# Attention over halves of the scores: the maximum in two parts on VectorE, and the scaled values on GpSimd

## The chip, the cores and the metric

The kernel runs on one core of one Trainium2 chip. The metric is the device time of one execution in microseconds (us); lower is better. Times given for a kernel are medians of several executions. The core has five engines that run their own queues of instructions in order: TensorE (PE, with its weight loads as PEld), VectorE (DVE), ScalarE (ACT), GpSimd (POOL) and SyncE (SP). They wait for each other by semaphores.

## What is computed

Two layers over x of shape 8 x 256 x 32 x 32, so 8 batches of 1024 tokens with 256 channels. The change lies in the attention of layer 0, which has 8 heads of 64 channels and takes its softmax over the queries (axis i), not over the keys:

```
qkv = (xt @ w_qkv + b_qkv).reshape(B, S, N_HEADS, 3 * D_K)
q, k, v = jnp.split(qkv, 3, axis=-1)
attn = jnp.einsum('bihd,bjhd->bijh', q, k) * SCALE
attn = jax.nn.softmax(attn, axis=1)
res = jnp.einsum('bijh,bjhd->bihd', attn, v).reshape(B, S, N_HEADS * D_K)
res = res @ w_out + b_out + xt
```

Layer 1 is an attention with one head over normalized tokens (`_L1_attn_ref`), added to its input, and a mixture of 8 experts, of which each token takes 2 (`_L1_ffn_ref`), added again.

## The kernel before

The outer loop runs over the 8 batches. A batch goes through `layer0` (the attention with 8 heads), `attend` (the attention of layer 1) and `dispatch` (router, ranks, and the scatter of the normalized tokens into a table of rows by expert: 16 indirect transfers on POOL's queue at line 610, and an addition on POOL at line 617). The batches form two groups, 0 to 6 and 7. When a group's last batch has been dispatched, `experts` runs its blocks of 256 rows. Its results are fetched back token by token in `results`: indirect transfers on POOL at line 800, products and sums on DVE at line 806, transposes on PE at line 817. For batches 0 to 6 this is done inside the `layer0` of batch 7.

In `layer0` the softmax axis is the queries. So the scores are made transposed: a tile has 128 keys on the partitions and 1024 queries along the free axis, and the maximum and the sum are taken along the free axis. There are 4 pairs of heads (g) and 8 blocks of 128 keys (j), so 32 steps (g, j) per batch. In a step:

- `score(at, h, n)`, line 323: one matmul for head h of the pair and half n (512 queries). Head 0 uses rows 0 to 63 of the array and head 1 rows 64 to 127, so matmuls of different heads run side by side. A score tile `psc` takes two PSUM banks, one for each half; there are 3 such buffers (`ps_big`).
- `soften(at, h)`: the negated maximum over 1024 queries on DVE (line 334), the exponential on ACT with the sum as accumulator output (line 336), and, for h = 1, the reciprocals of both sums (line 343) and the values times the reciprocals, `vs` (line 345), both on DVE.
- `gather_values(at)`, line 361: four matmuls that add the products of `vs` and the exponentials into `po`, two steps later (`LAG = 2`).

The loop at line 373 writes the order out by hand: the first half of head 0 stands beside the second half of head 1 of the step before, then the second half of head 0 beside the first half of head 1. After steps 3 and 5 of a pair, `project` (line 272, evicted on DVE at line 280) makes a query or key tile for the next pair in a buffer of the same pool. A scheduler places the instructions of each engine from this program, and puts in the semaphore waits.

Of the kernel before, what the change touches and what calls it, by code (L numbers as in the profile page):

```python
# [10 lines left out]
F32 = mybir.dt.float32  # L11
I32 = mybir.dt.int32
AF = mybir.ActivationFunctionType
ALU = mybir.AluOpType
AX = mybir.AxisListType
# [3 lines left out]
def kernel(  # L19
# [21 lines left out]
    nc = tc.nc  # L41
    P = 128
# [17 lines left out]
    const = ctx.enter_context(tc.tile_pool(name="const", bufs=1))  # L60
# [4 lines left out]
    small = ctx.enter_context(tc.tile_pool(name="small", bufs=6))  # L65
# [95 lines left out]
    nc.gpsimd.memset(later[:, :, 0:1], 0.0)  # L161

    wpack = dram.tile([E * P, WROW], F32, name="wpack")
    wbs = [const.tile([P, WROW], F32, name=f"wb_{i}") for i in range(NWB)]


    ps = acc("ps_bqk")
# [4 lines left out]
    ps = acc("ps_W")  # L172
# [7 lines left out]
    ps = acc("ps_r")  # L180
# [4 lines left out]
    ps = acc("ps_b1")  # L185
# [116 lines left out]
    def layer0(b, xT, between):  # L302

        v = values(b, xT)
        res = one.tile([P, NPAIR, S], F32, tag="res", name=f"res_{b}")
        qks = [[project(b, xT, 0, t) for t in range(2)]]
        if b == 0:  # L310
            prepare()
        steps = [(g, j) for g in range(NPAIR) for j in range(NT)]
        LAG = 2
        pss, exps, sums, vss = {}, {}, {}, {}
        po = None

        def score(at, h, n):
            g, j = steps[at]
            q, k = qks[g]
            if n == 0:  # L320
                pss[at, h] = big(f"psc_{b}_{g}_{j}_{h}")
            r = slice(h * DK, (h + 1) * DK)
            nc.tensor.matmul(  # L323
                pss[at, h][:, ts(n, 512)], k[r, ts(j, P)], q[r, ts(n, 512)], start=True, stop=True
            )

        def soften(at, h):

            g, j = steps[at]
            ps = pss.pop((at, h))  # L330
            if h == 0:
                sums[at] = small.tile([P, 2], F32, tag="sums", name=f"sums_{b}_{g}_{j}")
            nmax = small.tile([P, 1], F32, tag="nmax", name=f"nmax_{b}_{g}_{j}_{h}")
            nc.vector.tensor_reduce(nmax, ps, AX.X, ALU.max, negate=True)  # L334
            ex = expp.tile([P, 1024], F32, tag="exps", name=f"ex_{b}_{g}_{j}_{h}")
            nc.scalar.activation(  # L336
                ex, ps, AF.Exp, bias=nmax, scale=1.0, accum_out=sums[at][:, h : h + 1]
            )
            exps[at, h] = ex
            if h == 1:  # L340

                rs = small.tile([P, 2], F32, tag="rs", name=f"rs_{b}_{g}_{j}")
                nc.vector.reciprocal(rs, sums.pop(at))
                vs = four.tile([P, 2, DK], F32, tag="vs", name=f"vs_{b}_{g}_{j}")
                nc.vector.tensor_mul(  # L345
                    vs,
                    v[:, j, ts(g, P)].rearrange("p (h d) -> p h d", d=DK),
                    rs.unsqueeze(2).to_broadcast([P, 2, DK]),
                )
                vss[at] = vs  # L350

        def gather_values(at):
            nonlocal po
            g, j = steps[at]
            if j == 0:
                po = [acc(f"po_{b}_{g}_{n}") for n in range(NH2)]
            vs = vss.pop(at)
            exs = [exps.pop((at, h)) for h in range(2)]
            for n in range(NH2):
                for h in range(2):  # L360
                    nc.tensor.matmul(  # L361
                        po[n][h * DK : (h + 1) * DK, :],
                        vs[:, h, :],
                        exs[h][:, ts(n, 512)],
                        start=(j == 0),
                        stop=(j == NT - 1),
                    )
            if j == NT - 1:
                for n in range(NH2):
                    nc.scalar.copy(res[:, g, ts(n, 512)], po[n])  # L370

        last = len(steps) - 1
        for at in range(last + LAG + 1):
            if at <= last:
                score(at, 0, 0)
            if 0 < at <= last + 1:
                score(at - 1, 1, 1)
                soften(at - 1, 1)
            if at <= last:
                score(at, 0, 1)  # L380
                score(at, 1, 0)
                soften(at, 0)
            if at >= LAG:
                gather_values(at - LAG)
            if at <= last:
                g, j = steps[at]
                if j == NT - 1:
                    for group, item in between[g]:
                        results(group, [item])
                if g + 1 < NPAIR and j in (3, 5):  # L390
                    if j == 3:
                        qks.append([])
                    qks[g + 1].append(project(b, xT, g + 1, len(qks[g + 1])))


        t1 = one.tile([P, NT, C], F32, tag="t1", name=f"t1_{b}")
        for i in range(NT):
            pr = acc(f"pr_{b}_{i}")
            for g in range(NPAIR):
                nc.tensor.matmul(  # L400
                    pr[:, :C], res[:, g, ts(i, P)], wo[:, g, :], start=(g == 0), stop=False
                )
            for cc in range(NCC):
                nc.tensor.matmul(
                    pr[:, ts(cc, P)], xT[:, cc, ts(i, P)], ident, start=False, stop=(cc == NCC - 1)
                )
            nc.vector.tensor_add(t1[:, i, :], pr[:, :C], b_o)
        return t1


    def attend(b, t1):
        n1 = one.tile([P, NT, D], F32, tag="n", name=f"n1_{b}")
        layer_norm(t1, n1, 1e-5, f"a{b}")
        nT = one.tile([P, NCC, S], F32, tag="nT", name=f"nT_{b}")
        to_channels(n1, nT, f"n1_{b}")
        xa = one.tile([P, NCC, S], F32, tag="xa", name=f"xa_{b}")
        for ec in range(NCC):
            px = big(f"px_{b}_{ec}")
            for dc in range(NCC):
                for n in range(NH2):  # L420
                    nc.tensor.matmul(  # L421
                        px[:, ts(n, 512)],
                        WT[:, dc, ts(ec, P)],
                        nT[:, dc, ts(n, 512)],
                        start=(dc == 0),
                        stop=(dc == NCC - 1),
                    )
            nc.vector.tensor_copy(xa[:, ec, :], px)

        t2 = t1  # L430

        def scores(i):
            psc = big(f"ps1_{b}_{i}")
            for ec in range(NCC):
                for n in range(NH2):
                    nc.tensor.matmul(  # L436
                        psc[:, ts(n, 512)],
                        xa[:, ec, ts(i, P)],
                        nT[:, ec, ts(n, 512)],
                        start=(ec == 0),  # L440
                        stop=(ec == NCC - 1),
                    )
            nmax = small.tile([P, 1], F32, tag="nmax", name=f"nmax1_{b}_{i}")
            nc.vector.tensor_reduce(nmax, psc, AX.X, ALU.max, negate=True)  # L444
            ex = expp.tile([P, 1024], F32, tag="exps", name=f"ex1_{b}_{i}")
            ssum = small.tile([P, 1], F32, tag="ssum", name=f"ssum_{b}_{i}")
            nc.scalar.activation(ex, psc, AF.Exp, bias=nmax, scale=1.0, accum_out=ssum)  # L447
            return ex, ssum

        def mix(i, ex, ssum):  # L450
            pt = big(f"pa_{b}_{i}")
            for m in range(NT):
                nc.tensor.transpose(pt[:, ts(m, P)], ex[:, ts(m, P)], ident)
            aT = two.tile([P, S], F32, tag="tr", name=f"aT_{b}_{i}")
            nc.vector.tensor_copy(aT, pt)  # L455
            py = acc(f"py_{b}_{i}")
            for m in range(NT):
                nc.tensor.matmul(  # L458
                    py[:, :D], aT[:, ts(m, P)], n1[:, m, :], start=(m == 0), stop=(m == NT - 1)
                )  # L460
            rs = small.tile([P, 1], F32, tag="rs1", name=f"rs1_{b}_{i}")
            nc.vector.reciprocal(rs, ssum)
            nc.vector.scalar_tensor_tensor(  # L463
                t2[:, i, :], py[:, :D], rs, t1[:, i, :], ALU.mult, ALU.add
            )

        pending = None
        for i in range(NT):
            now = (i, *scores(i))
            if pending is not None:  # L470
                mix(*pending)
            pending = now
        mix(*pending)
        return t2
# [408 lines left out]
```

## Time and profile before

| | |
|---|---|
| median of 3 runs | 2899.07 us (2894.92 to 2901.2) |
| the profiled execution | 2900.13 us |
| its span, first to last instruction | 2898.4 us |
| mean granted TensorE clock | 0.943 |
| maximum over queries, line 334 | 512 instructions, 1219 ns each |
| exponentials, line 336 | 512 instructions, 1114 ns each |
| reciprocals, line 343 | 256 instructions, 165 ns each |
| values times reciprocals, line 345 | 256 instructions, 292 ns each |
| scatters, line 610 | 128 instructions on POOL, 974 ns each |

The profile is of one execution. Engines are named as above; "busy" is the time in which an engine runs an instruction. In the list of groups, a line gives the source line, the engine, the operation, what is written from what, the shapes and the count; after the first bar the busy time and the mean duration of one in ns; after the second the idle time of the engine just ahead of them and what ended most of it. In the timeline the columns are start, duration, engine, line and operation, and in brackets the idle time before and its releaser.

### The profile page before, as it was taken

The numbers are of one execution on the slowest core, as the hardware profiler recorded it, in microseconds if no ns is written. First come the engines' busy times: TensorE is split into PE (matmuls) and PEld (weight loads), VectorE is DVE, ScalarE is ACT, GpSimd is POOL, SyncE is SP. The second block draws the span as 40 slices with busy tenths as digits, with TensorE's granted clock in tenths as the row PEclk, the third lists the DMA queues.
The fourth block names the chain that finished last, engine by engine and source line by source line (L and its number), as shares of the span: only waits on it lengthen the run. The fifth ranks groups of instructions, "written<-read, shape, count | busy, mean of one in ns | idle before, by whom it ended". The sixth has DMA issues, their size and how long they took to land. (4 is left out here: it accounts for less than half of the span.)

```text
span 2898.4 us, 26495 instructions
## 1 busy us (share of the span) xinstructions
PE 2629.9 (91%) x10049; PEld 1379.7 (48%) x10049; DVE 1480.7 (51%) x2666; ACT 844.0 (29%) x1451; POOL 442.4 (15%) x445
## 2 busy tenths in 40 slices
PE   8999999999999999999999999999499988889946
PEld 3346434643464346434643464346377753224634
DVE  4664566456645664566456645664433335555422
ACT  2531253125312531253125312531011113332101
POOL 0000200020002000200020002000444442441043
PEclk9999999999999999999999999999699998879968
DMA  6984100010001000100010001000355532331044
GB/s 241 385 309 134 58 1 15 1 44 1 15 1 44 1 15 1 44 0 15 0 44 1 15 0 44 1 1 1 117 175 178 182 118 72 117 110 59 4 168 157
DMA packets 89304, 209.17 MB, mean 72 GB/s; under 512 B 16256, under 2 KB 22040, under 8 KB 87128
## 3 DMA queue, kind: packets, MB, share of 16 engines
q1 hardware_dynamic: 59272, 128.87, 12.3%
q0 software_dynamic: 29904, 78.61, 8.7%
q8 instruction: 79, 1.29, 0.2%
q14 instruction: 49, 0.40, 0.0%
HBM read 113.22 MB, written 126.36 MB: 83 GB/s over the span
## 5 line engine op out<-in xcount | busy, mean ns | idle before, releaser
L336 ACT ACTIVATE ex<-psc,nmax 128x1024 f32<-128x1024 f32 x512 | 570.5, 1114 | 846.8 <-DVE nmax L334 842.1
L334 DVE TENSOR_REDUCE nmax<-psc 128x1 f32<-128x1024 f32 x512 | 604.1, 1219 | 240.4 <-PE psc L323 240.2
L323 PE MATMUL psc<-qk,qk 64*128 64x512 f32 x2048 | 612.9, 645 | 35.4 <-DVE qk L280 20.7
L361 PE MATMUL po<-ex,vs 128*64 128x512 f32 x2048 | 508.8, 613 | 14.7 <-DVE vs L345 14.7
L323 PEld LDWEIGHTS psc<-qk,qk 64*128 64x128 f32 x2048 | 237.2, 191 | 377.6 <-ACT ex L336 162.0
L617 POOL TENSOR_TENSOR t<-t,n 128x2048 f32<-128x2048 f32 x8 | 36.1, 4511 | 1888.0 <-issue 1478.2
L361 PEld LDWEIGHTS po<-ex,vs 128*64 128x64 f32 x2048 | 127.2, 138 | 368.7 <-issue 307.5
L458 PE MATMUL py<-n,aT 128*128 128x256 f32 x1024 | 236.5, 384 | 11.2 <-DVE aT L455 11.2
L436 PE MATMUL ps<-nT,xa 128*128 128x512 f32 x512 | 236.9, 593 | 0.0
L272 PE MATMUL pqk<-xT,wqkv 128*128 128x512 f32 x512 | 233.9, 602 | 0.4 <-ACT ex L336 0.4
L458 PEld LDWEIGHTS py<-n,aT 128*128 128x128 f32 x1024 | 190.6, 190 | 67.3 <-DVE aT L455 43.9
L280 DVE TENSOR_SCALAR qk<-pqk,b_qk 128x1024 f32<-128x1024 f32 x64 | 82.1, 1283 | 180.3 <-PE pqk L272 180.3
L768 PE MATMUL pe<-wb,hb 128*128 128x256 f32 x624 | 156.1, 393 | 13.7 <-ACT hb L753 13.4
L447 ACT ACTIVATE ex<-ps,nmax 128x1024 f32<-128x1024 f32 x64 | 71.3, 1114 | 332.8 <-DVE nmax L444 325.1
L272 PEld LDWEIGHTS pqk<-xT,wqkv 128*128 128x128 f32 x512 | 93.4, 190 | 139.0 <-issue 99.2
L743 PE MATMUL ph<-xb,wb 128*128 128x256 f32 x624 | 152.7, 389 | 3.1 <-DVE xb L735 3.1
L800 POOL DMA_INDIRECT yk<-y,yat x128 | 123.8, 967 | 188.5 <-DVE o L806 97.4
L610 POOL DMA_INDIRECT rows<-n,d_at x128 | 124.6, 974 | 177.4 <-DVE row L597 125.5
L291 PE MATMUL pv<-wqkv,xT 128*128 128x512 f32 x256 | 142.0, 707 | 9.2 <-ACT wqkv L95 7.1
L753 ACT ACTIVATE hb<-ph,wb 128x256 f32<-128x256 f32 x156 | 65.5, 471 | 284.8 <-issue 241.2
L463 DVE SCALAR_TENSOR_TENSOR t<-py,rs,t 128x256 f32<-128x256 f32 x64 | 31.0, 484 | 228.2 <-PE py L458 228.2
L735 DVE COPY xb<-px 128x512 f32<-128x512 f32 x78 | 54.0, 692 | 157.5 <-PE px L733 157.5
(151 smaller groups left out, 2344.5 us busy)
## 6 DMA issues: line engine op xcount, KB each, us to landing
rows<-wb SPq DMA_DIRECT2D x8, 8192.0 KB, 51.3
y<-yb SPq DMA_DIRECT2D x78, 256.0 KB, 2.0
sums<-t SPq DMA_DIRECT2D x8, 1024.0 KB, 3.9
o<-sums SPq DMA_DIRECT2D x8, 1024.0 KB, 6.6
out_dram<-oT SPq DMA_DIRECT2D x16, 512.0 KB, 6.8
xT<-in_x_dram SPq DMA_DIRECT2D x7, 1024.0 KB, 6.0
wpack<-in_L_ffn_w_dram SPq DMA_DIRECT2D x4, 1024.0 KB
rows<-n,d_at POOLq DMA_INDIRECT x128, 2.4
```

The costliest lines, as they stand in the source:

```text
L272: nc.tensor.matmul(pq[:, ts(n, 512)], wqkv[:, cc, t, ts(g, P)], xT[:, cc, ts(n, 512)], start=(cc == 0), stop=(cc == NCC - 1),)
L291: nc.tensor.matmul(pv[:, ts(j, 512)], xT[:, cc, ts(i + j, P)], wqkv[:, cc, 2, :], start=(cc == 0), stop=(cc == NCC - 1),)
L323: nc.tensor.matmul(pss[at, h][:, ts(n, 512)], k[r, ts(j, P)], q[r, ts(n, 512)], start=True, stop=True)
L334: nc.vector.tensor_reduce(nmax, ps, AX.X, ALU.max, negate=True)
L336: nc.scalar.activation(ex, ps, AF.Exp, bias=nmax, scale=1.0, accum_out=sums[at][:, h : h + 1])
L361: nc.tensor.matmul(po[n][h * DK : (h + 1) * DK, :], vs[:, h, :], exs[h][:, ts(n, 512)], start=(j == 0), stop=(j == NT - 1),)
L436: nc.tensor.matmul(psc[:, ts(n, 512)], xa[:, ec, ts(i, P)], nT[:, ec, ts(n, 512)], start=(ec == 0), stop=(ec == NCC - 1),)
L458: nc.tensor.matmul(py[:, :D], aT[:, ts(m, P)], n1[:, m, :], start=(m == 0), stop=(m == NT - 1))
L610: nc.gpsimd.indirect_dma_start(out=view[:, :], out_offset=bass.IndirectOffsetOnAxis(ap=at[:, i : i + 1], axis=0), in_=n2[:, i, :], in_offs ...
L743: nc.tensor.matmul(ph[:, ts(fc, BR)], wb[:, dc * FF + fc * P : dc * FF + (fc + 1) * P], xb[:, dc, :], start=(dc == 0), stop=(dc == NCC - 1),)
L768: nc.tensor.matmul(py[:, ts(r, D)], hT[:, fc, ts(r, P)], wb[:, at + fc * D : at + (fc + 1) * D], start=(fc == 0), stop=(fc == NFC - 1),)
L800: nc.gpsimd.indirect_dma_start(out=yk[:, :], out_offset=None, in_=group.y[:, :], in_offset=bass.IndirectOffsetOnAxis(ap=ats[k][:, i : i + ...
```

## The change

The maximum of a score tile is taken in two parts. `first_max` reduces the first half (512 queries, one bank) with the same reduction as before. `soften` then runs one `tensor_scalar` over the second half: it multiplies by -1, takes the minimum with the first half's result, writes that to a scratch tile in SBUF that nobody reads, and gives the minimum over the free axis as its accumulator output. The score matmul of the second half would have to wait for `first_max`, because both use one tile; `declare_no_dep` tells the scheduler that they touch different banks, so no such wait is put in. `first_max` is called ahead of the second half's matmul. The product `vs` moves from DVE to POOL. In `attend` only the name of a tile changes.

```
+    scrap = const.tile([P, 512], F32, name="scrap")
...
-            nc.tensor.matmul(
+            mm = nc.tensor.matmul(
                 pss[at, h][:, ts(n, 512)], k[r, ts(j, P)], q[r, ts(n, 512)], start=True, stop=True
             )
+            if n == 1:
+                tc.declare_no_dep(mm.ins, firsts.pop((at, h)).ins, reason="the other bank")
+
+        def first_max(at, h):
+            g, j = steps[at]
+            nmax = small.tile([P, 1], F32, tag="nmax1", name=f"nmax1_{b}_{g}_{j}_{h}")
+            firsts[at, h] = nc.vector.tensor_reduce(
+                nmax, pss[at, h][:, ts(0, 512)], AX.X, ALU.max, negate=True
+            )
+            nmaxes[at, h] = nmax
...
-            nc.vector.tensor_reduce(nmax, ps, AX.X, ALU.max, negate=True)
+            nc.vector.tensor_scalar(
+                scrap,
+                ps[:, ts(1, 512)],
+                -1.0,
+                nmaxes.pop((at, h)),
+                ALU.mult,
+                ALU.min,
+                accum_out=nmax,
+            )
...
-                nc.vector.tensor_mul(
+                nc.gpsimd.tensor_mul(
                     vs,
...
             if at <= last:
+                first_max(at, 0)
                 score(at, 0, 1)
                 score(at, 1, 0)
                 soften(at, 0)
+                first_max(at, 1)
             if at >= LAG:
                 gather_values(at - LAG)
```

## The prediction

> **What bounds the kernel now.** The page comes first: which engine is full, and what the longest idle times of the others end on.
>
> ```profile
> PE 2629.9 (91%) x10049; PEld 1379.7 (48%) x10049; DVE 1480.7 (51%) x2666; ACT 844.0 (29%) x1451; POOL 442.4 (15%) x445
> L334 DVE TENSOR_REDUCE nmax<-psc 128x1 f32<-128x1024 f32 x512 | 604.1, 1219 | 240.4 <-PE psc L323 240.2
> ```
>
> TensorE (PE) works 91% of the span. The maximum that the change splits costs VectorE (DVE) 604 us, but DVE is half idle, so its busy time is no time to be won. What counts is the wait that ends last in the stage of the change. The timeline of a plain stretch of that stage (batch 1) shows it:
>
> ```profile
> 401.14 1.94 PE L361 MATMUL po<-ex,vs 128*64 128x512 f32 x8
> 403.01 2.17 PE L323 MATMUL psc<-qk,qk 64*128 64x512 f32 x8
> 404.18 2.36 DVE L334 TENSOR_REDUCE nmax<-psc 128x1 f32<-128x1024 f32 x2 [0.79 <-PE psc L323]
> 405.11 1.94 PE L361 MATMUL po<-ex,vs 128*64 128x512 f32 x8
> 405.50 1.11 ACT L336 ACTIVATE ex<-psc,nmax 128x1024 f32<-128x1024 f32 x1 [1.50 <-DVE nmax L334]
> 406.63 1.11 ACT L336 ACTIVATE ex<-psc,nmax 128x1024 f32<-128x1024 f32 x1
> 406.98 2.04 PE L323 MATMUL psc<-qk,qk 64*128 64x512 f32 x8
> 407.65 0.19 ACT L336 ACTIVATION_READ_ACCUMULATOR ex<-psc,nmax 128x1 f32 x1
> 407.89 0.29 PEld L323 LDWEIGHTS psc<-qk,qk 64*128 64x128 f32 x3 [0.19 <-ACT ex L336]
> 408.94 1.94 PE L361 MATMUL po<-ex,vs 128*64 128x512 f32 x8
> 410.81 2.17 PE L323 MATMUL psc<-qk,qk 64*128 64x512 f32 x8
> ```
>
> One step is a group of scores (L323) and a group of value products (L361). Two limits lie almost on each other. PE alone needs 1.96 us for a score group (406.98 to 408.94) and 1.87 for a value group (408.94 to 410.81): 3.83 a step. The other limit is a loop through three engines. From a group's start, 403.01, the first maximum starts 1.17 later and lasts 1.22; ScalarE (ACT) starts 0.10 after it, at 405.50, the second exponential follows at 406.63, and its accumulator is read by 407.84. Only then is its PSUM buffer free, and the second pair of scores of the next group starts at 407.89: 4.88 after 403.01. From there PE needs 2.92 to the group at 410.81. Two steps take 7.80, so 3.90 each. A shorter chain could save at most 0.07 a step.
>
> **The half maxima.** The order of instructions in the changed program keeps PE's sequence in batches 0 to 6, and its score matmuls wait for ACT alone, as before: the removed wait is the one that the new first maximum would have brought. DVE's order per step is: first half of (k, 0), second half of (k-1, 1), second half of (k, 0), first half of (k, 1), reciprocal. The matmuls that free the first two run as one pair and end together, so the useful second half stands behind a first half of another tile. Its rows:
>
> ```profile
> L654 DVE TENSOR_REDUCE p_e<-p_mine 128x63 f32<-128x504 f32 x1 | 0.7, 673 | 0.0
> L735 DVE COPY xb<-px 128x512 f32<-128x512 f32 x78 | 54.0, 692 | 157.5 <-PE px L733 157.5
> L617 POOL TENSOR_TENSOR t<-t,n 128x2048 f32<-128x2048 f32 x8 | 36.1, 4511 | 1888.0 <-issue 1478.2 <-DVE n L206 409.8
> ```
>
> First half: 0.68 (504 elements take 0.673), less 0.08 that two reductions in a row overlap (2.36 for two of 1.22): 0.60. Second half: between 0.69 (the copy of 512) and 0.75 (the tensor_scalar of line 280 takes 1.28 for 1024; 512 elements fewer save 0.53, the difference of copies of 1024 and 512, 1.225 and 0.692): 0.72. The accumulator output is not in the trace on DVE; on ACT the read adds 0.09 behind the activation. I take 0.09. Together 1.41 in place of 1.22: the chain is 0.19, say 0.2, **longer**. Bounds: 0.60 + 0.69 + 0 gives +0.07; 0.68 + 0.75, a whole small instruction of 0.17 (the reciprocal) and 0.04 for a wait on DVE's own semaphore give 1.64, +0.42. A gain is excluded here, since both halves wait for the same pair.
>
> The two-step loop becomes 7.80 + 0.2, so a plain step costs 0.10 more. A batch has 32 groups; between their starts lie 3 intervals of start-up, 6 pairs of 7.42 and 4.37 around the projections of line 272, and 16 plain ones of 3.90. The projection intervals absorb it: the group after a projection has 0.28 to 0.41 us to spare (at 426.61 PE starts, while the first exponential was read by 426.07). So 16 x 7 x 0.10 = **+11 us**. At +0.07 it is +4. At +0.42 another loop, group to first exponential to next group (2.49 + 1.21 + 0.05 = 3.75), becomes 4.17, 0.27 over 3.90: 30, and 4 more around projections, +34.
>
> [...]
>
> **The products on GpSimd (POOL).** In plain steps they are covered: a product is ready 0.39 us into the step that uses it (403.11 + 0.29) and PE takes it at 2.10 (405.11). Without that slack they would cost their own duration. What they are moved past is POOL's queue. In the changed order the products of batches 1 to 6 stand behind the 16 scatters of the batch before, and these run on into the new batch:
>
> ```profile
> 333.95 0.28 DVE L345 TENSOR_TENSOR vs<-v,rs 128x128 f32<-128x128 f32 x1
> 334.55 0.20 PEld L361 LDWEIGHTS po<-ex,vs 128*64 128x64 f32 x4 [1.30 <-DVE vs L345]
> 335.89 0.97 POOL L610 DMA_INDIRECT rows<-n,d_at  x1 [0.30 <-issue]
> ```
>
> The last scatter ends at 336.86, 2.31 after PE took the first product at 334.55; in batches 2 to 6 it is 2.34 to 2.43. The addition of line 617 stands ahead of the scatters in both orders. A product of 128 elements on POOL costs between 0.28 (4.511 x 128 / 2048) and 0.42 (with the 0.134 of POOL's smallest memset on top); I take 0.42, and 0.1 for hand-overs as between DVE and ACT. PE starts at 337.4, **2.85** late. Everything on PE stands behind it in order. While it waits, DVE and ACT stop too, for want of PSUM buffers, so nothing is caught up.
>
> The clock: after a 3.4 us stretch with PE 2.50 of 3.40 busy (327.4 to 330.8) the next stretch, 330.9 to 334.2, was granted 0.50, all others around it 1.00. A stall of 2.85 leaves PE emptier than that. A half-speed stretch costs up to 1.7; I take 1.2. Per batch 4.05, six times: **+24**. Low: 2.5 without the clock, +15; high: 2.85 + 0.6 + 1.7, +31.
>
> [...]
>
> **Ends of batches.** After the last group PE waits for a chain without cover (maximum at 474.57, value products at 477.76). There the second half alone stands on the path: 0.81 for 1.22, and the product 0.42 for 0.29. Net -0.28, eight times: **-2** (-3 to 0). The start of batch 0 gains and loses some 0.4.
>
> **Batch 7** takes gathered rows (line 800) through the same POOL queue, one each 1.26 us, and PE waits for them at lines 817. Some 12 of its 32 products stand between paced gathers, 0.7 each with the issue gap: 0 to 8. Two transposes also move back past score matmuls in PE's order, some us either way. I take **+3** (0 to 12).
>
> **Sum:** 11 + 24 - 2 + 3 = +36. The profiled execution took 2900.13 us, 1.7 around its span of 2898.4; the median is 2899.07, 1.1 below it, so I add to the median: **2935**. Low ends together: 4 + 15 - 3 + 0 = +16, 2915. High ends: 34 + 31 + 0 + 12 = +77, 2976.
>
> **Rivals.** (1) The start-up wait is hidden: POOL's scatters run earlier, or PE finds other work. Against it: the changed order puts nothing between. Then 11 - 2 + 3 = +12: 2911. (2) The chain is at its upper bound, because the accumulator read is a full instruction and DVE waits on itself, and batch 7 queues badly: 2960 to 2976. For it: the order shows the second half waiting for DVE as well as PE. (3) Faster: the mechanism is the split itself. If, in plain steps, DVE delivers the first maximum of a step earlier than after 1.22 us, that is, if both pieces together take less than that, the loop shrinks to PE's 3.83: 112 x 0.07 = -8, with -2 at the ends, -3 at the starts: 2886, provided POOL's wait stays away too. Against it: no 512-element row is below 0.67. (4) The change does nothing: the chain +0.07 and the wait hidden: about 2900.
>
> **Chances.** Forecast (2915 to 2955) 0.60; rival 1 0.12; rival 2 0.15; rival 3 0.06; rival 4 0.07. The time is the forecast's, 2935. The range reaches into rivals 1 and 2: 2908 to 2968. About 0.2%, 6 us, is what a measurement of this kernel can tell from no change. Faster 0.06, same 0.08 (rival 4 and the edge of rival 1), slower 0.86.
>
> **What would show it.** Plain steps of 4.00 instead of 3.90, with ACT's first exponential 2.7 after the group's start instead of 2.49. At the start of batches 1 to 6, PE idle about 3 us on a POOL product after the last scatter, and a further stretch at clock 0.5. The forecast is wrong if plain steps stay at 3.90 or fall, or if the first value group of batch 1 still starts about 9.2 us after its first scores.

## The result, and the profile after

| | before | after |
|---|---|---|
| median | 2897.05 us (4 runs, 2894.92 to 2901.2: the three above and one beside the changed kernel) | 2917.77 us (4 runs, 2913.8 to 2918.78) |
| ratio | | 1.0067, 95% interval 1.005 to 1.0085 |
| profiled execution, span | 2898.4 us | 2916.2 us |
| mean granted TensorE clock | 0.943 | 0.947 |

The change costs 20.7 us, 0.7%. These are the engines' line and the changed groups on the page of the changed kernel, and below them the group of value matmuls on the page of the kernel before:

```profile
PE 2631.1 (90%) x10049; PEld 1375.4 (47%) x10049; DVE 1481.8 (51%) x3434; ACT 837.4 (29%) x1451; POOL 544.1 (19%) x701
...
L382 PE MATMUL po<-ex,vs 128*64 128x512 f32 x2048 | 518.1, 624 | 35.4 <-POOL vs L366 35.4
L335 DVE TENSOR_REDUCE nmax<-psc 128x1 f32<-128x512 f32 x512 | 351.1, 687 | 260.4 <-PE psc L324 260.1
...
L347 DVE TENSOR_SCALAR_CACHE_REDUCE scrap<-psc,nmax 128x512 f32<-128x512 f32 x512 | 382.3, 747 | 59.8 <-PE psc L324 30.6
...
L366 POOL TENSOR_TENSOR vs<-v,rs 128x128 f32<-128x128 f32 x256 | 102.2, 401 | 1084.2 <-DVE rs L364 869.6
```

```profile
L361 PE MATMUL po<-ex,vs 128*64 128x512 f32 x2048 | 508.8, 613 | 14.7 <-DVE vs L345 14.7
```

Two pieces of the maximum take 687 and 747 ns where one took 1219, and DVE is as busy as before (1481.8 us against 1480.7), although 256 products of 0.29 us have left it. The line to look at is the first group: PE waits 35.4 us ahead of value matmuls, all of it for a product on POOL; before it was 14.7, for a product on DVE. In the trace, 23.1 of the 35.4 us lie at the starts of batches 1 to 6, where the kernel before has no such wait; the ends of batches and batch 7 hold the rest.

One of these starts, that of batch 1 after the change, in the timeline:

```profile
332.79 0.16 DVE L364 RECIPROCAL rs<-sums 128x2 f32<-128x2 f32 x1
...
333.31 0.96 POOL L633 DMA_INDIRECT rows<-n,d_at  x1 [0.30 <-DVE rs L364]
...
334.58 0.97 POOL L633 DMA_INDIRECT rows<-n,d_at  x1 [0.30 <-issue]
335.57 0.76 POOL L366 TENSOR_TENSOR vs<-v,rs 128x128 f32<-128x128 f32 x2
336.03 0.29 PEld L382 LDWEIGHTS po<-ex,vs 128*64 128x64 f32 x4 [4.55 <-POOL vs L366]
336.03 3.68 PE L382 MATMUL po<-ex,vs 128*64 128x512 f32 x8 [3.72 <-POOL vs L366]
...
341.66 0.69 DVE L335 TENSOR_REDUCE nmax<-psc 128x1 f32<-128x512 f32 x1 [8.12 <-PE psc L324]
```

Even the reciprocal of the second step has been there since 332.95. Two products stand behind POOL's last scatters, which end at 335.55, and run at once, 335.57, both together in 0.76. PE has waited 3.72 us. Then its eight matmuls take 3.68 where eight took 1.94 in a plain stretch before, and DVE gets its next scores 8.12 us after its last work. The windows of the granted clock over the same stretch (columns: window, its length, then PE's, PEld's, DVE's, ACT's and POOL's busy time with the number of instructions, granted TensorE clock, DMA share, GB/s) say why:

```profile
327.74:331.15 3.41, 2.98 (x8) 1.24 (x8) 3.19 (x9) 2.74 (x6) 2.50 (x4) 1.00 0.27 94
331.16:334.57 3.41, 1.15 (x5) 0.32 (x3) 2.12 (x5) 2.41 (x4) 2.50 (x3) 1.00 0.28 99
334.57:337.98 3.41, 1.95 (x6) 0.72 (x8) 0.00 (x0) 0.00 (x0) 1.73 (x3) 0.50 0.22 77
337.98:341.39 3.41, 3.41 (x10) 0.90 (x8) 0.00 (x0) 0.00 (x0) 0.00 (x0) 0.50 0.00 0
```

PE is busy 1.15 us of the stretch from 331.16, and the next two stretches are granted 0.50.

The plain steps of batch 1 after the change:

```profile
403.75 1.99 PE L324 MATMUL psc<-qk,qk 64*128 64x512 f32 x8
...
404.92 0.69 DVE L335 TENSOR_REDUCE nmax<-psc 128x1 f32<-128x512 f32 x1 [1.30 <-PE psc L324]
405.52 0.74 DVE L347 TENSOR_SCALAR_CACHE_REDUCE scrap<-psc,nmax 128x512 f32<-128x512 f32 x1
...
406.19 0.08 DVE L347 DVE_READ_ACCUMULATOR scrap<-psc,nmax 128x1 f32 x1
406.37 1.11 ACT L357 ACTIVATE ex<-psc,nmax 128x1024 f32<-128x1024 f32 x1 [1.93 <-DVE scrap L347]
...
407.48 1.10 ACT L357 ACTIVATE ex<-psc,nmax 128x1024 f32<-128x1024 f32 x1
407.63 0.30 PEld L324 LDWEIGHTS psc<-qk,qk 64*128 64x128 f32 x4 [0.90 <-ACT ex L357]
```

From the first piece to the first exponential it is now 1.45 us (404.92 to 406.37), against 1.32 before (404.18 to 405.50). The accumulator read is a row of its own, 0.08 us. The first exponential starts 2.62 after the group, where it was 2.49, and the next group, at 407.63, waits for it. Two plain steps take 7.89 (403.75 to 411.64) for 7.80.

To see where the time went as a whole, the span is cut by PE's records, for batches 0 to 6: from a batch's first scores to the start of its fourth group (start-ups), from there to its last group (the 28 later steps), from that to its last value matmul (ends), and from there to the next batch's first scores (gaps: the rest of layer 0, layer 1 and the router; six of them). The last column is the rest: batch 7, with the experts before and after it. About 38 us lie ahead of the first scores in each and are in no column. From its first scores to its last value matmul a batch is in its head, as it is called below.

| us | span | start-ups | later steps | ends | gaps | rest |
|---|---|---|---|---|---|---|
| before | 2898.4 | 77.8 | 932.2 | 66.7 | 814.8 | 968.6 |
| after | 2916.2 | 103.5 | 943.9 | 65.3 | 800.4 | 964.8 |
| split alone | 2883.4 | 70.0 | 940.4 | 63.9 | 806.3 | 964.5 |
| POOL products alone | 2916.6 | 103.3 | 932.7 | 68.3 | 802.8 | 971.0 |
| after, first products on DVE | 2891.4 | 70.0 | 940.2 | 65.4 | 812.1 | 965.6 |
| split alone, order turned | 2856.1 | 70.4 | 925.5 | 63.6 | 802.2 | 956.8 |
| the same, later products on POOL | 2864.6 | 70.4 | 925.6 | 65.1 | 799.9 | 965.1 |
| split at starts and ends only | 2880.2 | 70.0 | 934.3 | 64.8 | 803.8 | 969.4 |
| before, one matmul more | 2883.9 | 69.7 | 932.0 | 66.7 | 804.5 | 973.1 |
| before, delayed once | 2904.0 | 76.6 | 932.1 | 66.8 | 818.8 | 972.3 |
| before, again | 2900.0 | 76.7 | 932.0 | 66.7 | 815.2 | 972.0 |
| after, wait kept | 3138.6 | 113.7 | 1105.2 | 72.0 | 816.1 | 993.0 |

Between before and after, start-ups cost 25.7, later steps 11.7, ends give 1.4, gaps 14.3 and the rest 3.9: +17.8 in the spans (the medians differ by 20.7; this profiled execution of the kernel before is one of its longer ones). The gaps, whose code the change hardly touches, are the surprise.

### The profile page after: what moved, and what is told of

It is laid out like the page before. It is cut to its first block, busy times and chain, and to the rows that moved or that the text cites. A ratio compares the mean times of both kernels' runs of the same rounds, so it can differ in the third digit from the quotient of the medians.

```text
span 2916.2 us, 28469 instructions
## 1 busy us (share of the span) xinstructions
PE 2631.1 (90%) x10049; PEld 1375.4 (47%) x10049; DVE 1481.8 (51%) x3434; ACT 837.4 (29%) x1451; POOL 544.1 (19%) x701
## 5 line engine op out<-in xcount | busy, mean ns | idle before, releaser
L382 PE MATMUL po<-ex,vs 128*64 128x512 f32 x2048 | 518.1, 624 | 35.4 <-POOL vs L366 35.4
L335 DVE TENSOR_REDUCE nmax<-psc 128x1 f32<-128x512 f32 x512 | 351.1, 687 | 260.4 <-PE psc L324 260.1
L347 DVE TENSOR_SCALAR_CACHE_REDUCE scrap<-psc,nmax 128x512 f32<-128x512 f32 x512 | 382.3, 747 | 59.8 <-PE psc L324 30.6
L366 POOL TENSOR_TENSOR vs<-v,rs 128x128 f32<-128x128 f32 x256 | 102.2, 401 | 1084.2 <-DVE rs L364 869.6
L791 PE MATMUL pe<-wb,hb 128*128 128x256 f32 x624 | 156.1, 393 | 13.7 <-ACT hb L776 13.4
```

What stands on the lines that cost most here:

```text
L335: firsts[at, h] = nc.vector.tensor_reduce(nmax, pss[at, h][:, ts(0, 512)], AX.X, ALU.max, negate=True)
L347: nc.vector.tensor_scalar(scrap, ps[:, ts(1, 512)], -1.0, nmaxes.pop((at, h)), ALU.mult, ALU.min, accum_out=nmax,)
L382: nc.tensor.matmul(po[n][h * DK : (h + 1) * DK, :], vs[:, h, :], exs[h][:, ts(n, 512)], start=(j == 0), stop=(j == NT - 1),)
L791: nc.tensor.matmul(py[:, ts(r, D)], hT[:, fc, ts(r, P)], wb[:, at + fc * D : at + (fc + 1) * D], start=(fc == 0), stop=(fc == NFC - 1),)
```

## The experiments

Edits are against the kernel named. Ratios are to the kernel before, run beside it on the same chip: 2899.61 us for the first four experiments below, 2900.75 for the run with one matmul more and for the last one, 2901.96 for the others.

**The split alone** (the changed kernel with its product back on DVE):

```
-                nc.gpsimd.tensor_mul(
+                nc.vector.tensor_mul(
```

> The halves of the maximum as in the change, the products of values back on VectorE. My theory (two separate causes): the longer chain alone is here. Plain steps average 3.94 to 3.95 us as in the changed kernel, the steps with a projection 7.50 instead of 7.42, the first value products of batches 1 to 6 start at most 9.3 us after the first scores, since no product stands behind a scatter. The layer-0 heads grow by about 1 us each, 7 to 9 us in all without batch 7; what lies between the heads may give some of it back through the clock, 0 to 14 us. Time: 2890 to 2905. Rival (the wait for GpSimd is what lengthens the chain, through the reciprocal that waits on GpSimd): plain steps go back to 3.90.

Measured: 2886.21 us (2882.38 to 2889.84), ratio 0.9962, interval 0.9948 to 0.9977. The split by itself makes the kernel faster, and more so than expected. Its plain steps are slower, as in the changed kernel (112 of 3.94 instead of 3.90, +4.6, and 42 projection intervals of 7.50 instead of 7.42, +3.6); ends give 2.8 back, since only the second piece stands on their path; start-ups give 7.8 and gaps 8.5. Where these two come from is followed up below.

**The POOL products alone** (the kernel before with the product on POOL):

```
-                nc.vector.tensor_mul(
+                nc.gpsimd.tensor_mul(
```

> The maximum in one reduction as before, only the products of values on GpSimd. My theory: plain steps stay at 3.90 and projection steps at 7.42; in batches 1 to 6 the first value products start about 12.1 us after the first scores instead of 9.25, and the start-up (first three intervals) grows from 11.1 to about 15.5 us, 27 us in all. Between the heads the clock gives back 0 to 14 us. Time: 2908 to 2925. Rival (start-up is lost to the split order, not to the queue): start-up stays at 11.1 and the time at 2897.

Measured: 2917.61 us (2912.14 to 2921.45), ratio 1.0065, interval 1.0049 to 1.0081: the loss of the whole change. Start-ups of batches 1 to 6 take 15.0 to 15.6 us instead of 11.1; plain steps stay at 3.90. POOL's part is the loss and nothing but start-ups carries it. The two parts don't add: -13.4 and +18.0 would make +4.6, and the change has +20.7. What the split wins at a start-up is spent waiting for the same scatters: the start-ups are 103.3 without the split and 103.5 with it.

**The changed kernel with the products of a batch's first three steps on DVE:**

```
-                nc.gpsimd.tensor_mul(
+                mul = nc.vector if at < 3 else nc.gpsimd
+                mul.tensor_mul(
```

> The changed kernel with the products of the first three steps of each batch on VectorE and the other 29 on GpSimd. My theory: the start-up stall behind the scatters is gone, the first value products start at most 9.3 us after the first scores, start-up falls from 15.6 to 11.1 us or a little less; plain steps stay at 3.94. Time between 2890 and 2905. Rival (products on GpSimd cost in every step, or the scatters still hold the fourth product): start-up or the steps after it stay long and the time stays above 2908.

Measured: 2892.51 us (2887.82 to 2895.19), ratio 0.9977, interval 0.9967 to 0.9987. 24 of 256 products moved back take 25 us off. Start-ups are those of the split alone, 70.0, and the other 232 products cost 1.5 us at the ends (9.33 for 9.11 each) and nothing in the steps. Of the 24, the 18 in batches 1 to 6 stood behind scatters. So it is the queue behind the scatters, not POOL's slower product, that the change pays for. Batch 0, which has no scatters ahead of it, says the same inside the changed kernel's own trace: its start-up takes 9.95 us.

**The kernel before, delayed once** by some 2 us in batch 0, to see whether the gaps depend on where a batch falls on the grid on which the granted clock changes (in the clock records of the kernel before and of the changed kernel, every change lies within 0.003 us of a multiple of 3.4133 us from the first record):

```
+        if b == 0:
+            for _ in range(7):
+                nc.vector.tensor_scalar_mul(n1[:, NT - 1, :], n1[:, NT - 1, :], 1.0)
```

> The kernel before with seven multiplications by 1 on VectorE ahead of the transposes of batch 0 in layer 1, a delay of about 2 us once. My theory: the granted clock is set anew every 3.41 us, on a grid that does not move with the program; in the kernel before a batch takes 290.11 us, almost exactly 85 such stretches, so that all six batches meet the grid at the same point and each has four half-speed stretches between its head and the next. The delay moves all of them at once: the gap after the head of batch 1 falls from 136.3 us to 133 or less, and the sum of the gaps after batches 1 to 5 by 5 to 20 us; the time falls below that of the kernel before by 3 to 18 us although work was added. Rival (the shorter gaps of the changed kernel come from its own instructions or transfers): the gaps stay at 136.3 and the time rises by about 2 us.

Measured: 2900.21 us (2896.52 to 2905.73), ratio 1.0004, interval 0.9996 to 1.0013. The expected gain did not come. No gap became shorter; all six took 136.2 to 136.9 (the first of them holds the delay itself). The delay didn't last either: two batches later heads and gaps lay on the grid as in the first profile. A batch of the kernel before takes 290.1 us, which is 85 stretches of 3.413, and returns to the same place. One batch went against the pattern: batch 1, which fell 0.9 us later on the grid, had no half-speed stretch in its start-up and took 9.96 us for it, without any split.

**The kernel before, profiled again**, to tell what belongs to an execution and what to the kernel:

> The kernel before, profiled a second time. In the first profile the gaps between the batches' heads (last value group to the next batch's first scores) were 133.2, then 136.3 five times, 814.8 in all, with 2, 4, 4, 4, 4, 4 stretches at half clock; the changed kernel's were 800.4 with 1, 4, 3, 2, 4, 1. Theory 'the half-speed stretches of a gap belong to the execution, not to the kernel': here the counts differ from 2, 4, 4, 4, 4, 4 and the gaps' sum moves by 3 to 15 us. Rival 'they follow from the kernel': the same counts in nearly all gaps and a sum of 813 to 817, so that the 14 us which the changed kernel has less there belong to the change.

Measured: 2901.67 us, one run. Five gaps of 136.2 to 136.4 with 4 half-speed stretches each and a sum of 815.2, as the first time. Batch 0 alone fell differently: start-up 9.90 without a half-speed stretch, for 11.14 with one. So the rival holds: what a gap takes follows from the kernel, given where its batch falls on the grid. Over all 12 profiles, 72 gaps, the length goes with the place on the grid at which the head before it ends (the start of its last value matmul, modulo 3.413 us, counted from the first clock record): from 1.15 to 2.9, 43 of 44 gaps take 135.4 to 136.9; elsewhere 27 of 28 take 131.4 to 133.8. The number of half-speed stretches in a gap goes with its length too: with 1 to 3 of them 28 gaps take 131.4 to 133.8, with 4 of them 44 gaps take 134.3 to 136.9. So where a head ends on the grid goes with up to 5 us in the gap behind it, in either kernel. That is an association over all profiles; no run placed a gap on purpose and got what was foretold.

**DVE's order turned.** In the split alone, DVE takes the first half of (k, 0) ahead of the second half of (k-1, 1), though both become ready together and ACT needs the second half first. One line of order turns them (`seconds` keeps the second-half instructions):

```
-                first_max(at, 0)
+                if at > 0:
+                    with tc.issue_after(seconds[at - 1, 1].ins):
+                        first_max(at, 0)
+                else:
+                    first_max(at, 0)
```

> The split as in the first run, products on DVE, but in DVE's order the second half of (k-1, 1) stands ahead of the first half of (k, 0), so that both maxima that the first pair of matmuls frees are taken in the order in which ACT needs them. Theory 'DVE order': the split run's plain steps take 3.944 because the chain maximum start to first exponential is 1.45 us; with the order turned, the first exponential starts 0.85 after DVE starts, the second is ready after 0.75 + 0.69 + 0.75 + 0.17 = 2.36, so the second exponential starts about 3.55 after the group's start against 3.73 in the split run: 0.18 for two steps, plain steps of 3.85 (PE's own 3.83 is the floor), projections back at 7.42. Time 2886 - 112 x 0.09 - 3.4 = 2873 to 2878. Rival 'the split is slow wherever it stands': plain steps stay at 3.92 to 3.95 and the time at 2884 to 2890, because two pieces cost DVE 1.45 in any order. Rival 'start-up pays': plain steps fall, but the start-ups of the seven batches grow by 0.7 each and eat half of it, 2878 to 2882.

Measured: 2860.47 us (2857.96 to 2864.5), ratio 0.987, interval 0.985 to 0.9889: faster than both kernels. Plain steps take 3.845, the projection intervals 7.42 again, start-ups stay at 10.0. The timeline of one step, batch 1:

```profile
396.85 1.99 PE L325 MATMUL psc<-qk,qk 64*128 64x512 f32 x8
...
398.03 0.75 DVE L348 TENSOR_SCALAR_CACHE_REDUCE scrap<-psc,nmax 128x512 f32<-128x512 f32 x1 [1.14 <-PE psc L325]
398.71 0.08 DVE L348 DVE_READ_ACCUMULATOR scrap<-psc,nmax 128x1 f32 x1
398.71 0.68 DVE L336 TENSOR_REDUCE nmax<-psc 128x1 f32<-128x512 f32 x1
...
398.89 1.11 ACT L358 ACTIVATE ex<-psc,nmax 128x1024 f32<-128x1024 f32 x1 [1.56 <-DVE scrap L348]
...
400.37 1.11 ACT L358 ACTIVATE ex<-psc,nmax 128x1024 f32<-128x1024 f32 x1 [0.28 <-DVE rs L365]
400.64 0.30 PEld L325 LDWEIGHTS psc<-qk,qk 64*128 64x128 f32 x4 [0.81 <-ACT ex L358]
```

The first exponential starts 0.86 after DVE begins, and 2.04 after the group instead of 2.62; the second starts at 3.52, where 3.55 was expected. Here the split shortens the chain, as its form promises. The time is 13 us below the expected 2873: the steps were sized rightly (14.9 for 13.5), and the gaps (4), batch 7 and what follows it (8) came on top.

**The split in a batch's first three and last two steps only:**

```
         def first_max(at, h):
+            if 3 <= at < last - 1:
+                return
...
+            if (at, h) in nmaxes:
...
+            else:
+                nc.vector.tensor_reduce(nmax, ps, AX.X, ALU.max, negate=True)
```

> The split only in the first three and the last two steps of a batch, one maximum over 1024 elsewhere, products on DVE. Theory 'the split helps only where PE has no cover': start-ups stay at 10.0 in batches 1 to 6 (the split run) against 11.1 before, tails at 9.2 to 9.4 against 9.5, while projection intervals go back from 7.50 to 7.42 and plain steps from 3.944 to 3.903; 2886.2 - 3.6 - 4.6 = 2878. Rival 'the gain of the split run lies in the clock of the gaps between the batches': the stage gains 8 us as said but the gaps come out at 814 as before, and the time at 2884 to 2890. Rival 'the start-up gain needs the split in all steps': start-ups go back to 11.1 and the time to 2893 to 2899.

Measured: 2877.78 us (2875.99 to 2882.47), ratio 0.9926, interval 0.9911 to 0.9941; expected 2878. The start-ups keep their 70.0, so the gain there needs the split only there. The later steps cost 2.1 over the kernel before (one interval per batch at the change of form), not 8.2.

**One matmul more.** A start-up of the kernel before lasts 11.1 us with a half-speed stretch and 9.9 without one, and the split's start-up is no shorter than that, 10.0. So the split might win there through the clock alone: its windows show PE busier ahead of the stretch in question. To separate the clock from the maxima, the kernel before got a score matmul of 256 columns, whose result nobody reads, early in the start-up, where PE later idles 0.90 us:

```
+                if at == 1:
+                    fill = acc(f"fill_{b}")
+                    q, k = qks[0]
+                    nc.tensor.matmul(
+                        fill[:, :256], k[0:DK, 0:P], q[0:DK, 0:256], start=True, stop=True
+                    )
```

> The kernel before with one more score matmul of 256 columns per batch, whose result nobody reads, early in the start-up, where PE later idles 0.90 us for a score buffer. Theory 'the split shortens the start-ups through the clock': before, the 3.41 us stretch from 327.4 had PE busy 2.51 and the next one was granted 0.50; in the split run the same stretch had 2.98 and the next one stayed at 1.00, and the three first steps took 10.0 for 11.1. The extra matmul of about 0.43 lifts the stretch to about 2.94, so the half-speed stretch is gone, the first three steps take 9.9 to 10.2 in batches 0 to 6, and 7 x 1.1 = 7.7 us are won by more work: 2888 to 2895, less if gaps between batches shorten too, beside 2900 before. Rival 'the split shortens the start-up through its own chain': the half-speed stretch is not a matter of PE's idle time, the start-ups stay at 11.1 or grow by the 0.43 of the extra matmul, 2899 to 2904.

Measured: 2883.82 us (2882.66 to 2889.3), ratio 0.9951, interval 0.9934 to 0.9967. More work, less time, and less than the 2888 to 2895 that were expected with gaps as before; the gaps shortened too. These are the windows at the start of batch 2 of three kernels, with the grid at the same place; first the kernel before, then the split alone, then the kernel before with one matmul more:

```profile
617.60:621.02 3.42, 2.52 (x7) 0.89 (x6) 3.33 (x3) 2.25 (x4) 2.51 (x4) 1.00 0.27 95
621.02:624.43 3.41, 3.41 (x9) 1.70 (x7) 1.59 (x3) 1.43 (x4) 2.80 (x3) 0.50 0.33 115
```

```profile
614.07:617.48 3.41, 2.98 (x8) 1.04 (x6) 3.29 (x9) 2.05 (x3) 2.50 (x4) 1.00 0.27 93
617.48:620.90 3.42, 3.42 (x12) 1.25 (x12) 3.22 (x10) 2.80 (x7) 2.81 (x3) 1.00 0.33 115
```

```profile
613.44:616.85 3.41, 2.94 (x10) 1.15 (x7) 3.31 (x3) 2.25 (x4) 2.50 (x4) 1.00 0.23 81
616.85:620.27 3.42, 3.42 (x15) 1.44 (x15) 2.67 (x4) 2.47 (x6) 2.73 (x3) 1.00 0.33 115
```

Read the second number (PE busy) of the first line and the clock (third from the end) of the second. With PE busy 2.52 of 3.41 the next stretch was granted 0.50; with 2.98 and 2.94 it was granted 1.00. All seven start-ups lost their half-speed stretch and took 9.90 to 9.96 us, -8.1 together. Not all seven show the matmul's effect. Batches 0, 2, 4 and 6 begin 1.13 to 1.25 us into a stretch of the grid, where every start-up of the kernel before has a half-speed stretch; the other three begin 2.23 to 2.24 us into one, where the kernel before has none (batch 1 of the delayed run, 2.16). In the four profiles without the split or the extra matmul, the 22 start-ups that begin at 0.74 to 1.67 have that stretch and the 6 that begin at 1.76 to 2.22 don't. All seven of the split alone begin at 1.04 to 1.24 and have none. The gaps fell to 804.5 with the start-ups, three of 131.8 and three of 136.3 to 136.4, which is more of the gain than the start-ups themselves. PE's busy time in one stretch doesn't settle it: in the delayed run a stretch with 2.51, lying 0.9 us earlier in the start-up, was not followed by half speed, and in the kernel before the stretch from 324.06 with 2.15 was followed by 1.00 and the one from 586.88 with 3.42 by 0.50. What does settle it is not shown.

In the clock records of the kernel before, the granted clock is 1.00 or 0.50 and nothing between; it falls to 0.50 in 37 places, and its mean over the span is 0.943. The 0.5% won here are nearly as much as the 0.7% that the whole change costs.

**The wait kept.** The changed kernel without its declaration, so that the score matmul of the second half waits for the first half's maximum:

```
-            if n == 1:
-                tc.declare_no_dep(mm.ins, firsts.pop((at, h)).ins, reason="the other bank")
```

> The changed kernel with the scheduler's own dependence left in: the score matmul of the second half waits until the first half's maximum has been taken. Theory 'the declaration takes away a real wait, one that the split brings': the matmul that now starts about 0.98 us after its group has to wait until the first pair has ended (1.17), the maximum has been taken (0.69) and a hand-over of 0.05 has passed, 1.9 in all, so 0.9 more in each of the 224 steps, +200 us, 3100 to 3130, and PE idle on DVE at the score line. Rival 'DVE was waiting there anyway and PE has room': plain steps of 4.0 to 4.2, 2930 to 2970. Rival 'no effect, the hardware orders it anyway': 2915 to 2921.

Measured: 3140.28 us, one run, 222.5 above the changed kernel, a little over the 3100 to 3130 expected. The page of this kernel names the wait:

```profile
L324 PE MATMUL psc<-qk,qk 64*128 64x512 f32 x2048 | 690.4, 686 | 192.0 <-DVE nmax L332 152.7
```

The later steps take 0.82 more each ((1105.2 - 943.9) / 196), 161 us. So the declaration is what makes the split bearable; it takes away a wait that only the split brings.

**The order turned, and the products from the fourth step on at POOL** (the two edits above together):

> The split with DVE's order turned, as in the fastest run so far (2860), and the products of all steps but a batch's first three on GpSimd. Theory 'the products are covered except at the starts': the plain steps stay at 3.84 to 3.85 and the projection intervals at 7.42, the tails grow by 0.2 each as between the split run (9.11) and the run with its first products on DVE (9.33), start-ups stay at 10.0; 2860 + 2 = 2862, 2857 to 2868 with the gaps' clock. Rival 'GpSimd frees DVE and the loop shortens further': plain steps at 3.83 and 2850 to 2857. Rival 'the slower product is no longer covered once steps are shorter': plain steps at 3.87 or more, 2870 or more.

Measured: 2863.48 us (2862.03 to 2866.33), ratio 0.9876, interval 0.9858 to 0.9893. Steps are the same to 0.1 us in all, ends cost 1.5 more; the rest is 8.3 longer in the two profiles, and the gaps 2.3 shorter. Even with POOL's wait avoided, the second half of the change has nothing to give: taking the products off DVE makes no step shorter.

## Why the prediction came out as it did

The predicted time was 2935 in a range of 2908 to 2968, with slower at 0.86; 2917.77 was measured. Direction, mechanism and place were right. By terms:

- **POOL's queue at the starts of batches, +24.** The queue is right, and shown by two runs (the products alone carry the loss, the first three moved back remove it). PE's first value group was to come 2.85 later; measured from the first scores it came 12.11 us after them in batches 2 to 6 instead of 9.25, which is 2.86. The clock was put at 1.2 per batch, at most 1.7, and that was too little. From the first value group to the next group it is now 3.28 to 3.61 us, mostly at half speed, where it was 1.87: 1.6 more a batch inside the start-ups, which grew by 4.5 each (26.9 in all, less 1.2 in batch 0). The half-speed stretches also reach past the start-ups: the next interval takes up to 8.6 us where the split alone takes 7.50, 3.3 us over the six batches, which the table counts under later steps. Together the clock took 2.2 a batch and this term 30, not 24. The further stretch that was forecast came in batches 1, 4 and 6; in the others one stretch came as before, but later, on the value group.
- **The chain, +0.2 a pair of steps, +11.** Right in sign, too large for plain steps, and the covered place was not covered. The first exponential was to start 2.7 after the group and started 2.62 after it: the chain grew by 0.13, because the second piece holds the path for 0.67 (0.72 taken) and the accumulator's read is 0.08, of which 0.07 overlaps the piece before it. The pair of steps grew by 0.09, plain steps by 0.04 instead of 0.10: 4.8 us. "The projection intervals absorb it" failed: they grew from 7.42 to 7.50 (3.6 us in the split alone). The slack of 0.28 to 0.41 that was read there belongs to the group behind the projection, not to the interval itself. The two mistakes largely cancel: 8.2 in the split alone, and 8.4 of the 11.7 that the later steps cost in the changed kernel.
- **The accumulator.** Its read was taken as 0.09, from the one on ACT. On DVE the read has its own row of 0.08 us.
- **Products on POOL.** 0.401 each, for 0.42 taken; on DVE one took 0.292, so POOL's takes 1.37 times as long. The loss comes from the queue ahead of them and not from this: the 232 products of the later steps cost 1.5 us at POOL.
- **Ends, -2.** Measured -1.4: -0.4 a batch by the second piece, +0.2 by POOL's product.
- **Batch 7, +3.** Not resolved. The batch's own stretch gave 3.8 in the changed kernel's profile, but the kernel before differs by 2.8 between its two profiles there.
- **Gaps, 0.** This is the step that failed. The prediction had no term for the stages between the heads, since their instructions stay as they are. They gave 14.3 us. The likely cause is the clock: the length of a gap goes with the place on the clock's grid at which it begins, and the longer start-ups moved the batches off the place to which a period of 290.1 us kept them. No run placed a gap on purpose, so this cause is not shown. Without the gaps the terms sum to +32, against +36 predicted; that closeness is partly luck, since the clock came out larger than predicted, and the chain, batch 0 and the rest smaller.
- **Start of batch 0, "gains and loses some 0.4".** It gained 1.2, as in the split alone. But the kernel before took 9.90 there in its second profile, where batch 0 fell elsewhere on the grid, so this 1.2 comes through the clock and not through shorter work. That a filled idle spot of PE could take a half-speed stretch away was not seen, though the prediction had the row (2.50 of 3.40 busy, then 0.50) and used it only to price the stall.

By its time alone 2917.77 lies nearer to rival 1 (2911, the start-up wait hidden) than to 2935. The traces decide against it: PE waits 3.72 us for a product on POOL in batch 1.

Rival 3, the split as a gain where POOL's wait stays away, was put at 2886, and the split alone measured 2886.21. The agreement is of the number only: it was to come from plain steps at 3.83, which went up to 3.94 instead; start-ups at full clock and shorter gaps gave it. In the order that the rival needed, with the second half first, plain steps fell to 3.845 and the time to 2860. "A gain is excluded here, since both halves wait for the same pair" holds for the order that the changed kernel has, not for the split.

## What to carry to other kernels

Before an operation is moved to an idle engine, look at what stands ahead of it in that engine's queue at each change of stage: the products of three steps, queued behind 16 scatters at each batch's start, cost all that was lost, the 232 others 1.5 us. When a reduction is split so that a part can start early, issue the parts in the order in which the consumer needs them: here one order took plain steps from 3.90 us to 3.94, the other to 3.845, and the kernel became 1.3% faster than before. Look at the granted clock behind an idle spot of TensorE too: here a stretch with PE busy 1.15 of 3.41 us was followed by two at 0.50, in a kernel that fills TensorE to nine tenths. And compare the stages that were not touched: the gaps took 14.3 us less after the change.

## What the runs showed of the hardware

- A matmul that nobody needs, once per batch in an idle spot of 0.9 us, won 0.5%. At the start of batch 2 PE was busy 2.94 instead of 2.52 us of a stretch, and the next 3.41 us were granted 1.00 instead of 0.50; over the run the start-ups gave 8.1 us and the gaps behind them 10.3.
- In the changed kernel the granted clock changed only at multiples of 3.4133 us from its first record, while the batches began at 0.76 to 3.17 us after one. The batches of the kernel before follow each other at 290.1 us, 85 stretches: delayed once by 2 us, they were back at their place on the grid after two batches. Five of its six gaps took 136.2 to 136.4 us; over all 12 profiles, 27 of the 28 gaps behind heads that ended elsewhere on the grid took 131.4 to 133.8.
- In the changed kernel a reduction with an accumulator output took 0.75 us for 512 elements on DVE, a plain reduction 0.69, and the accumulator's read 0.08, of which 0.07 beside the piece before.
- Two products of 128 elements in a row on POOL took 0.76 together, one alone 0.40.
